# Squares of two of the four outer outputs summed over embeddings by ScalarE, in segments of 64 with its accumulator output, in place of a square on ScalarE and a reduction on VectorE

## The chip, the cores and the metric

The kernel runs on one core of a Trainium2 chip. A core has several engines that work side by side, each with its own in-order queue of instructions: TensorE (PE, matmul), VectorE (DVE), ScalarE (ACT), GpSimd (POOL) and SyncE (SP, which here issues transfers). They share an on-chip memory (SBUF) and an accumulation memory for matmul results (PSUM), and they wait for each other through semaphores. The metric is the device time of one execution in microseconds (us), smaller being better.

## The reference

It is a factorization-machine layer in float32, with 64 embeddings, 512 features, 512 outputs and a batch of 1024:

```python
out_lin = x @ lin_w.T + lin_b
xv = jnp.einsum('bf,efm->bem', x, weight)
zp = jnp.einsum('bf,efm->bem', jnp.square(x), jnp.square(weight))
interaction = 0.5 * jnp.sum(jnp.square(xv) - zp, axis=1)
return out_lin + interaction
```

For each batch row and output column m, the product x times weight is taken for all 64 embeddings e, squared, and summed over e. The sum over e of the squared weights enters through one small product at the end (`zp`).

## The kernel before

**Tiling.** The large product is 1024 x 512 by 512 x (512 outputs x 64 embeddings). The columns are cut into NG = 16 weight groups of 32 outputs x 64 embeddings. In a group the product is done by two levels of a seven-product (Strassen-Winograd) scheme: the outer level makes seven products of blocks, run in the order `ORDER = (1, 6, 2, 7, 4, 5, 3)`, called trees here; inside each tree `tree()` makes seven inner products (`product()`, L433), each as matmuls into a pair of PSUM banks. A tile such as `oa0`, `ob0` or `c_0` is 128 partitions x 2 x 512: G = 2 blocks of batch rows, and in each 512 columns, which are MI = 8 outputs x E = 64 embeddings with the embedding running fastest.

**What a tree does.** Its inner products 5 and 3 go to PSUM tile `b3`, product 1 to `b1`, and ScalarE copies these out: `p5` and `p53` from `b3`, `b2` from `b1` (`copy`, L445, which is L287 in the profile). TensorE then adds products 6, 7 and 4 onto the copied `b2` and product 2 onto `b1`. PLACE sets where each inner product stands on TensorE relative to its tree: product 5 at -6, product 3 at -2, product 1 at 0, up to product 4 at 9, so the trees overlap. Product 3 accumulates onto `b3` only after the copy `p5` has been taken. Then VectorE and GpSimd combine the results into the outer tiles (`outer_psum` and `outer_sbuf`; the two-input adds are L274 in the profile). The inner right-hand sides `t` are made by GpSimd (L426).

**The squares.** When an outer output block is complete, `finish()` (L402) is called for it. This happens in the trees i = 2, 3, 4 and 5, which complete o11, o12, o21 and o22, for each of four positions `pos`. `finish()` squares the tile in place on ScalarE (L289) and then reduces it on VectorE over the 64 embeddings (L296), 128x1024 to 128x16, into the group's accumulator tile `acc`. Tree 4 has its output in a ring of three tiles `c`, tree 3 in `ob0` to `ob3`, trees 2 and 5 in `oa0` to `oa3`. The squares of the weights (`wsq`) take the same two steps in `w_squares()`. At the end of a group `acc` is sent to DRAM; that of the last group is read directly by the additions at L546. After the last group, four banks of closing matmuls (L565) make the `zp` term; VectorE adds it, and the result goes out.

**What sets the order.** Nothing is issued as it is written. Every operation is entered in a `Plan` with a cost for each engine that may run it, its reads and its writes. `Plan.order()` (L62) fixes TensorE's order by key, works latest times back from it, and then simulates all queues: each engine takes the ready operation with the earliest latest time. Some adds may go to VectorE or GpSimd, whichever the planner finds free. The costs are constants in the code: 1.04 for a PSUM copy, 1.07 for a square, 1.14 for a reduction. The resulting sequence is emitted with the engines' in-order queues, so a wrong cost moves no work between engines at run time; it only makes an instruction wait, with all behind it in its queue.

Of the kernel before, what the change touches and what calls it, by code (L numbers as in the profile page):

```python
# [12 lines left out]
AF = mybir.ActivationFunctionType  # L13
# [4 lines left out]
G = 2  # L18
# [5 lines left out]
PE, DVE, ACT, POOL, SP = "PE", "DVE", "ACT", "POOL", "SP"  # L24
# [150 lines left out]
def kernel(  # L175
# [27 lines left out]
    nc = tc.nc  # L203
    NG, NQ, _, NCB, KH, N = weight.shape
# [5 lines left out]
    MI = MG // 4  # L210
    E = N // MI
# [13 lines left out]
    buf = {}  # L225
# [36 lines left out]
    plan = Plan()  # L262
# [3 lines left out]
    def two_input(o, a, b, sub, size=1024, psum=False):  # L266

        costs = {DVE: 0.08 + 1.06 * size / 1024}
        if not psum:
            costs[POOL] = 0.14 + 2.19 * size / 1024  # L270

        def emit(e):
            f = engines[e].tensor_sub if sub else engines[e].tensor_add
            f(o, a, b)  # L274

        return costs, emit
# [7 lines left out]
    def act(o, i, func, reads, writes, cost=1.04):  # L284
        def emit(_):
            if func is None:
                nc.scalar.copy(o, i)  # L287
            else:
                nc.scalar.activation(o, i, func)  # L289

        plan.add({ACT: cost}, emit, reads, writes)

    def reduce(o, i, reads, writes):
        plan.add(
            {DVE: 1.14},
            lambda _: nc.vector.tensor_reduce(  # L296
                o, i.rearrange("p a (m e) -> p a m e", e=E), axis=AX.X, op=ALU.add
            ),
            reads, writes,
        )  # L300
# [17 lines left out]
    for k in range(NK):  # L318
        q, r = divmod(k, KH)
        for g, bank in enumerate(lin_banks):  # L320
            h = g // 2

            def emit(_, k=k, q=q, r=r, g=g, h=h, bank=bank):
                for j in range(G):
                    nc.tensor.matmul(  # L325
                        buf[bank][:, j, :],
                        buf[f"oa{2 * h + q}"][:, r, ts((g * G + j) % (NB // 2), P)],
                        buf[f"ob{q}"][:, r, :],
                        start=(k == 0),
                        stop=(k == NK - 1),  # L330
                    )
# [3 lines left out]
    for g, bank in enumerate(lin_banks):  # L335
        o = ("ob2", "ob3", "c_0", "c_1")[g]
        for j in range(G):
            costs, emit = two_input(buf[o][:, j, :], buf[bank][:, j, :], bias, False, 512, True)
# [3 lines left out]
    def block4(i):  # L342
        return buf[f"X{i}"][:, 0:4, :].rearrange("p (k q) b -> p k (q b)", k=2)
# [8 lines left out]
    def a_ap(n):  # L352
        return buf[a_buf[n]] if n in a_buf else block4(int(n[1]))
# [3 lines left out]
    for i, a, b, sub in ((5, "A21", "A22", 0), (6, "X5", "A11", 1), (7, "A11", "A21", 1), (3, "A12", "X6", 1)):  # L357
        costs, emit = two_input(block4(i), a_ap(a), a_ap(b), sub)
        plan.add(costs, emit, a_parts(a, b), (f"X{i}",), both=True)
    for i in ORDER:  # L360
# [3 lines left out]
        for o, a, b, sub in ((s1, a21, a22, 0), (s2, s1, a11, 1), (s4, a12, s2, 1), (a21, a11, a21, 1)):  # L364
            costs, emit = two_input(o, a, b, sub, 256)
# [36 lines left out]
    def finish(g, i, n, pos):  # L402

        row, col = {2: (0, 0), 3: (0, 1), 4: (1, 0), 5: (1, 1)}[i]
        q, cc = divmod(pos, 2)
        b, m = (row * 2 + q) * G, (col * 2 + cc) * MI
        act(buf[n], buf[n], AF.Square, (n,), (n,), 1.07)
        reduce(buf[acc_name[g]][:, b:b + G, m:m + MI], buf[n], (n,), ((acc_name[g], i, pos),))

# [1 line left out]
    TARGET = {1: "oa", 6: "ob", 2: "oa", 7: "oa", 3: "ob"}  # L411
    RHS = {1: "w11", 2: "w21", 3: "w22", 4: "w21", 5: "T1", 6: "T2", 7: "w12"}
    acc_name = {}
    acc_parts = [(i, pos) for i in (2, 3, 4, 5) for pos in range(4)]

    def tree(s, g, i):
        r = [f"{w(g, RHS[i])}.{c}" for c in range(NCB)]
# [33 lines left out]
        def outer_psum(b, pos):  # L451

            if i == 1:
                copy(f"oa{pos}", b)
            elif i == 5:
                for n in (f"oa{pos}", f"ob{pos}"):
                    whole(n, n, b, psum=True)
                finish(g, i, f"oa{pos}", pos)
            else:
                o = target(pos)  # L460
                whole(o, b, f"{ADDEND[i]}{pos}", psum=True)
                if i in (2, 4, 3):
                    finish(g, i, o, pos)

        def outer_sbuf(b, p, pos):

            if i == 1:
                whole(f"oa{pos}", b, p, psum=True)
            elif i == 5:
                whole(p, b, p, psum=True)  # L470
                for n in (f"oa{pos}", f"ob{pos}"):
                    whole(n, n, p)
                finish(g, i, f"oa{pos}", pos)
            else:
                a, o = f"{ADDEND[i]}{pos}", target(pos)
                z = p if o == a else o
                whole(z, b, p, psum=True)
                whole(o, z, a)
                if i in (2, 4, 3):
                    finish(g, i, o, pos)  # L480
# [41 lines left out]
    last = acc_name[NG - 1]  # L522
# [5 lines left out]
    for g in range(NB // G):  # L528
        n, a = lin_all[g], acc_all[g]
# [12 lines left out]
    def add_acc(g, lo, hi, a, reads):  # L542
        l = buf[lin_all[g]][:, :, lo:hi]
        plan.add(
            {DVE: 0.15 + 1.09 * (hi - lo) / N},
            lambda _: nc.vector.scalar_tensor_tensor(l, a, 0.5, l, ALU.mult, ALU.add),  # L546
            reads + (lin_all[g],), (lin_all[g],),
        )
# [2 lines left out]
        add_acc(g, 0, edge, buf[acc_all[g]][:, :, 0:edge], (acc_all[g],))  # L551
    for g in range(NB // G):
        rows = {0: (2, 3), 1: (4, 5)}[g // 2]
        reads = tuple((last, i, 2 * (g % 2) + c) for i in rows for c in range(2))
        add_acc(g, edge, M, buf[last][:, ts(g, G), :], reads)

    out_dst = out.rearrange("(n p) m -> p n m", p=P)
# [1 line left out]
    for g, bank in enumerate(("b3", "b1", "b2_0", "b2_1")):  # L559
        o = acc_all[g]  # L560
        h = g // 2
        for j in range(G):
            def emit(_, bank=bank, g=g, h=h, j=j):
# [10 lines left out]
            costs, emit = two_input(  # L574
                buf[o][:, j, :], buf[bank][:, j, :], buf[lin_all[g]][:, j, :], False, 512, True
            )
# [37 lines left out]
```

## Time and profile before

| | |
|---|---|
| median of 3 runs | 1438.39 us (1438.19 to 1439.19) |
| profiled execution, its span | 1436.8 us |
| PE busy | 1408.8 us (98%) |
| DVE busy | 1245.7 us (87%) |
| POOL busy | 1149.6 us (80%) |
| ACT busy | 748.8 us (52%) |

The span is the profiled execution's own time from the first to the last instruction. "Busy" is the time in which an engine has an instruction running. In the rows below, a line of the profile names the source line of the kernel, the engine, the operation, the tiles (out<-in, buffer numbers left out), the shapes, how often (x), then busy time and mean duration in ns, and after the second bar the idle time of that engine just before those instructions with what ended it. The chain of waits gives start and duration of each piece of the work that set the end, followed back from the last instruction; "issue" is time in which nothing seen in the profile is waited for.

### The profile page before, as it was taken

The page shows a single profiled execution, that of the slowest core. Times are in us where ns is not written, and L with a number is a line of the kernel's source. Part 1 is how long each engine was busy: PE and PEld are TensorE (multiplying, and loading weights), DVE is VectorE, ACT ScalarE, POOL GpSimd, SP SyncE. Part 2 cuts the span into 40 slices and gives each one's busy share as a digit, 9 for nine tenths or more (in the row PEclk, how much of TensorE's full clock was granted, in tenths as well). Part 3 has the DMA queues.
Part 4 walks back from the last instruction along what each step waited for, and adds up shares of the span by engine and source line. Part 5 has one row for each costly group of instructions (what it writes and reads, how often), then busy time and mean ns, then how long its engine had stood idle before and what let it go on. Part 6 is the DMA issues. An engine that isn't in the chain of part 4 may idle for free.

```text
span 1436.8 us, 10763 instructions
## 1 busy us (share of the span) xinstructions
PE 1408.8 (98%) x3264; PEld 619.3 (43%) x3264; DVE 1245.7 (87%) x1006; ACT 748.8 (52%) x756; POOL 1149.6 (80%) x691
## 2 busy tenths in 40 slices
PE   7999999999999999999999999999999999999998
PEld 3444444444444444444444444444444444444443
DVE  1899898998989899898988989899898888989984
ACT  1465554645545465564556555465554546556441
POOL 6988886878878688896878888687887868889781
PEclk9999999999999999999999999999999999999999
DMA  5311111111111112111111111111111111210221
GB/s 212 117 60 58 48 59 33 59 48 59 59 42 51 33 59 62 46 58 33 59 48 58 59 48 59 33 59 48 58 59 45 53 32 57 60 52 22 88 74 59
DMA packets 40377, 83.54 MB, mean 58 GB/s; under 512 B 18240, under 2 KB 19264, under 8 KB 40320
## 3 DMA queue, kind: packets, MB, share of 16 engines
q1 hardware_dynamic: 39664, 81.54, 18.1%
q10 hardware_dynamic: 576, 1.05, 0.2%
q8 instruction: 27, 0.44, 0.1%
q14 instruction: 30, 0.25, 0.1%
q0 software_dynamic: 80, 0.26, 0.0%
HBM read 76.68 MB, written 6.16 MB: 58 GB/s over the span
## 4 chain that ended last, share of the span: by engine, by line
PE 90%; POOL 4%; DVE 2%; issue 1%; ACT 1%; DMA 1%; DVEq 0%; POOLq 0%; SPq 0%
PE b L438 86%; POOL oa L274 3%; PE b L325 2%; PE b L565 2%; ACT p L287 1%; POOL t L274 1%; DMA ob<-lin_wT 0%; DVE p L274 0%; DMA T1.1_83<-lind 0%; DVE ob L274 0%; DVE w11.1_73 L536 0%; DVE w21.0_76 L274 0%; DVE oa L274 0%; DVE acc L296 0%; DVE w11.0_72 L536 0%
## 5 line engine op out<-in xcount | busy, mean ns | idle before, releaser
L438 PE MATMUL b<-t,X 128*128 128x512 f32 x1792 | 806.2, 592 | 2.0 <-DVE p L274 1.6
L438 PEld LDWEIGHTS b<-t,X 128*128 128x128 f32 x1792 | 340.0, 190 | 431.9 <-issue 415.0
L287 ACT COPY p<-b 128x1024 f32<-128x1024 f32 x224 | 225.6, 1007 | 266.1 <-PE b L438 226.8
L289 ACT ACTIVATE oa<-oa 128x1024 f32<-128x1024 f32 x128 | 131.9, 1054 | 165.3 <-DVE oa L274 90.9
L296 DVE TENSOR_REDUCE w_sum<-wsq 128x16 f32<-128x1024 f32 x128 | 154.8, 1211 | 29.0 <-ACT wsq L289 28.9
L287 ACT COPY b<-b 128x1024 f32<-128x1024 f32 x112 | 111.8, 998 | 91.1 <-PE b L438 85.2
L274 DVE TENSOR_TENSOR p<-b,p 128x1024 f32<-128x1024 f32 x96 | 117.0, 1218 | 43.4 <-PE b L438 43.4
L296 DVE TENSOR_REDUCE acc<-oa 128x16 f32<-128x1024 f32 x128 | 152.0, 1207 | 0.0
L438 PE MATMUL b<-w21.0_76,X 128*128 128x512 f32 x256 | 120.3, 592 | 0.0
L274 POOL TENSOR_TENSOR oa<-oa,p 128x1024 f32<-128x1024 f32 x32 | 102.8, 3212 | 1.8
L289 ACT ACTIVATE c<-c 128x1024 f32<-128x1024 f32 x64 | 67.7, 1058 | 67.8 <-DVE c L274 67.8
L274 POOL TENSOR_TENSOR oa<-p,oa 128x1024 f32<-128x1024 f32 x32 | 75.7, 2365 | 27.2 <-DVE p L274 26.9
L274 DVE TENSOR_TENSOR oa<-b,p 128x1024 f32<-128x1024 f32 x64 | 78.0, 1219 | 11.7 <-PE b L438 10.8
L274 POOL TENSOR_TENSOR c<-c,oa 128x1024 f32<-128x1024 f32 x32 | 75.4, 2357 | 13.8 <-DVE c L274 11.7
L274 POOL TENSOR_TENSOR oa<-oa,ob 128x1024 f32<-128x1024 f32 x32 | 76.4, 2387 | 6.9 <-DVE oa L274 6.9
L274 POOL TENSOR_TENSOR ob<-ob,oa 128x1024 f32<-128x1024 f32 x32 | 76.3, 2384 | 5.5 <-DVE ob L274 5.5
L274 POOL TENSOR_TENSOR t<-w21.0_76,t 128x512 f32<-128x512 f32 x32 | 40.8, 1275 | 48.3 <-PE b L438 48.3
L274 POOL TENSOR_TENSOR ob<-p,ob 128x1024 f32<-128x1024 f32 x32 | 75.7, 2364 | 0.5 <-DVE p L274 0.5
L296 DVE TENSOR_REDUCE acc<-ob 128x16 f32<-128x1024 f32 x64 | 75.9, 1209 | 0.0
L296 DVE TENSOR_REDUCE acc<-c 128x16 f32<-128x1024 f32 x64 | 74.8, 1208 | 1.1 <-ACT c L289 1.1
L438 PEld LDWEIGHTS b<-w21.0_76,X 128*128 128x128 f32 x256 | 48.6, 190 | 61.2 <-issue 61.2
L274 DVE TENSOR_TENSOR ob<-b,oa 128x1024 f32<-128x1024 f32 x32 | 39.1, 1223 | 40.5 <-PE b L438 39.8
(127 smaller groups left out, 2295.9 us busy)
## 6 DMA issues: line engine op xcount, KB each, us to landing
w11.0_72<-weight SPq DMA_DIRECT2D x16, 512.0 KB, 3.7
w11.1_73<-weight SPq DMA_DIRECT2D x16, 512.0 KB, 3.8
w12.0_74<-weight SPq DMA_DIRECT2D x16, 512.0 KB, 3.8
w12.1_75<-weight SPq DMA_DIRECT2D x16, 512.0 KB, 3.8
w21.0_76<-weight SPq DMA_DIRECT2D x16, 512.0 KB, 3.8
w21.1_77<-weight SPq DMA_DIRECT2D x16, 512.0 KB, 4.7
w22a.0_78<-weight SPq DMA_DIRECT2D x8, 512.0 KB, 3.8
w22a.1_79<-weight SPq DMA_DIRECT2D x8, 512.0 KB, 3.8
```

The source lines that it names most:

```text
L274: f(o, a, b)
L287: nc.scalar.copy(o, i)
L289: nc.scalar.activation(o, i, func)
L296: lambda _: nc.vector.tensor_reduce(o, i.rearrange("p a (m e) -> p a m e", e=E), axis=AX.X, op=ALU.add),
L325: nc.tensor.matmul(buf[bank][:, j, :], buf[f"oa{2 * h + q}"][:, r, ts((g * G + j) % (NB // 2), P)], buf[f"ob{q}"][:, r, :], start=(k == 0) ...
L438: nc.tensor.matmul(buf[b][:, j, :], buf[f"X{i}"][:, SLOT[p], ts(j, P)], op, start=first, stop=True, skip_group_check=True,)
L565: nc.tensor.matmul(buf[bank][:, j, :], buf[xe[h, k // KH]][:, k % KH, ts((g * G + j) % (NB // 2), P)], w2_sum[:, k, :], start=(k == 0), st ...
```

## The change

In trees 3 and 4 `finish()` no longer squares the whole tile and reduces it. It cuts the tile into 2 x 8 segments of 64 columns, one for each row block j and output, and squares each with one ScalarE instruction whose accumulator output is written to the output's place in `acc`. Four segments at a time are one entry of the plan, booked at 0.83 us, so a tile makes four entries. Trees 2 and 5, and the squares of the weights, stay as they were. The list of the parts of `acc` that the transfer and the last additions wait for is extended to match.

```diff
@@ finish
         b, m = (row * 2 + q) * G, (col * 2 + cc) * MI
+        if i in (3, 4):
+            for j in range(G):
+                for h in range(2):
+                    def emit(_, j=j, h=h):
+                        for u in range(MI // 2):
+                            v = h * (MI // 2) + u
+                            o = buf[n][:, j, ts(v, E)]
+                            nc.scalar.activation(
+                                o, o, AF.Square,
+                                accum_out=buf[acc_name[g]][:, b + j, m + v:m + v + 1],
+                            )
+
+                    plan.add({ACT: 0.83}, emit, (n,), ((acc_name[g], i, pos, j, h),))
+            return
         act(buf[n], buf[n], AF.Square, (n,), (n,), 1.07)
         reduce(buf[acc_name[g]][:, b:b + G, m:m + MI], buf[n], (n,), ((acc_name[g], i, pos),))
@@
-    acc_parts = [(i, pos) for i in (2, 3, 4, 5) for pos in range(4)]
+    acc_parts = [(i, pos) for i in (2, 5) for pos in range(4)] + [
+        (i, pos, j, h) for i in (3, 4) for pos in range(4) for j in range(G) for h in range(2)
+    ]
@@
-        reads = tuple((last, i, 2 * (g % 2) + c) for i in rows for c in range(2))
+        reads = tuple(
+            (last, *k) for k in acc_parts if k[0] in rows and k[1] // 2 == g % 2
+        )
```

In the changed kernel the segments are line 414. Because the planner makes the order anew from the costs, other instructions on ScalarE, VectorE and GpSimd change places as well; their number and tiles stay the same but for the 128 reductions and 128 whole-tile squares that are gone.

## The prediction

> **What bounds the kernel now.** I read the page first (engines, clock, chain), then the stages, then the chain in order of time.
>
> ```profile
> span 1436.8 us, 10763 instructions
> ...
> PE 1408.8 (98%) x3264; PEld 619.3 (43%) x3264; DVE 1245.7 (87%) x1006; ACT 748.8 (52%) x756; POOL 1149.6 (80%) x691
> ...
> PEclk9999999999999999999999999999999999999999
> ```
>
> TensorE is busy for 98% of the span at a granted clock in the top tenth throughout. ScalarE (ACT), the engine that gets the new work, has the most room on average: 52%. An average hides where work is bunched, so I cut out one of the 16 weight groups:
>
> ```profile
> core 0: us, PE busy (x) PEld busy (x) DVE busy (x) ACT busy (x) POOL busy (x), PEclk, DMA share, GB/s
> ...
> 207.13:292.32 85.19, 84.37 (x197) 37.15 (x196) 76.25 (x62) 46.51 (x48) 69.91 (x42) 1.00 0.17 52
> ```
>
> A group lasts 85.19 us, 84.37 of it matmul. With seven trees in a group that is 84.37 / 7 = 12.05 us of PE per tree. The other 0.8 us is one stop, which the chain shows:
>
> ```profile
> 207.13 1.00 ACT p L287
> 208.13 0.04 issue
> 208.17 79.25 PE b L438 x184
> 287.42 0.03 POOLq L274
> 287.45 0.59 POOL t L274
> 288.04 3.30 POOL oa L274
> 291.34 0.02 issue
> 291.36 0.02 ACT oa L289
> 291.38 0.94 issue
> 292.32 1.00 ACT p L287
> 293.33 0.04 issue
> ...
> 1404.63 27.48 PE b L565 x64
> ```
>
> At the end of each group POOL's last `oa` add ends at 291.34. Only then can ACT square that `oa`, and the copy of `b3` into `p5` at 292.32 stands behind this square in ACT's queue. PE waits for the copy. The wait seen from PE, summed over 16 groups:
>
> ```profile
> L438 PE MATMUL b<-w11.1_73,X 128*128 128x512 f32 x64 | 31.7, 618 | 13.4 <-ACT p L287 13.4
> ```
>
> So what can be gained in the groups is at most 13.4 us; what can be lost has no such bound, since the copies that PE waits for and the squares share one in-order queue.
>
> **The change, part by part.** Removed: per group, the four `c` squares of tree 4 and the four `ob` squares of tree 3, with a reduction each.
>
> ```profile
> L289 ACT ACTIVATE c<-c 128x1024 f32<-128x1024 f32 x64 | 67.7, 1058 | 67.8 <-DVE c L274 67.8
> L289 ACT ACTIVATE ob<-ob 128x1024 f32<-128x1024 f32 x64 | 67.6, 1059 | 4.8 <-POOL ob L274 1.6 <-DVE ob L274 0.5
> ...
> L296 DVE TENSOR_REDUCE acc<-ob 128x16 f32<-128x1024 f32 x64 | 75.9, 1209 | 0.0
> L296 DVE TENSOR_REDUCE acc<-c 128x16 f32<-128x1024 f32 x64 | 74.8, 1208 | 1.1 <-ACT c L289 1.1
> ```
>
> DVE loses 75.9 + 74.8 = 150.7 us, 9.4 of its 76.25 per group. I credit nothing for it beyond the 13.4 us bound: in the chain above, DVE isn't what PE waits for, and a group can't be shorter than its 84.37 us of matmul. What hides DVE's work now is that matmul stream; it has 8.9 us of DVE idle per group before, more after.
>
> Added on ACT: 128 sets, each cut into G x MI = 16 squares of 128x64, so 2048 squares. In the built program each is followed by an instruction of its own that reads the accumulator out, so 4096 new instructions stand where 128 stood. The planner books 0.83 us for four squares, 0.2075 each. No DMA is issued or moved past anything else's data: SP's transfers keep their buffers, and POOL and PE keep the same instructions.
>
> *Steps of the large ones.* ACT overlaps neighbours a little, so I take start to start:
>
> ```profile
> 246.75 0.99 ACT L287 COPY p<-b 128x1024 f32<-128x1024 f32 x1
> 247.64 1.06 ACT L289 ACTIVATE oa<-oa 128x1024 f32<-128x1024 f32 x1
> ...
> 265.36 1.06 ACT L289 ACTIVATE wsq<-w11.0_72 128x1024 f32<-128x1024 f32 x1
> 266.31 1.04 ACT L289 ACTIVATE wsq<-w22b.1_81 128x1024 f32<-128x1024 f32 x1
> ```
>
> A copy takes 0.89 us of the queue (I use 0.90), a square 0.95 of its 1.06: some 0.10 us of a record lies under the next.
>
> *One segment, c us: a square of 64 and its read.* The trace has no ACT instruction this short and no accumulator read, so I bound both. Low: 0.95 x 64/1024 = 0.06 for the square with no fixed part, and 0.10 for the read, the piece of a record that the square alone would have hidden; c = 0.16. High: the nearest short rows are DVE's.
>
> ```profile
> L546 DVE SCALAR_TENSOR_TENSOR T1.1_83<-w22a.1_79,T1.1_83 128x960 f32<-128x960 f32 x1 | 1.1, 1145 | 0.0
> L546 DVE SCALAR_TENSOR_TENSOR w21.1_77<-acc,w21.1_77 128x64 f32<-128x64 f32 x1 | 0.2, 216 | 0.0
> ```
>
> From 960 to 64 elements the record falls by 929 ns over 896 elements, 1.04 ns each, so 216 - 66 = 150 ns is fixed. Two such records end to end, 0.216 + 0.216, with 0.02 for the hand-over (the "issue" pieces of the chain), give c = 0.45. I take one short record plus one fixed part, c = 0.216 + 0.150, less a little for overlap: **c = 0.36**. I lean to the high end because the read needs the finished sum of the square just ahead, and the next square can't add into the accumulator before it is read: the overlap that the 1024-wide rows show should be mostly lost.
>
> The Trainium skill ("ScalarE: Activation LUTs", section What ACT_TABLE_LOAD costs) gives an ACTIVATE with immediate operands 186 ns + 0.833 ns per element, neighbours overlapping by 93 ns. For 1024 elements that is 1039 ns and a step of 946, and the trace agrees (1058 and 950). It has no price for the read; taken as one more instruction of one element, an estimate from that page is 146 + 94 = 240 ns for c, and the sum below would come to about 1459. "Perfetto Trace Analysis" of the Trainium skill, section Optimizing Scalar/DVE Operations, puts about 93 ns of fixed busy time on a ScalarE operation on SBUF: 3968 more instructions would be an estimated 369 us more on ACT, 748.8 + 369 = 1118 of 1437, so read on the average that rule sees no loss; no row here has a short ACT instruction to test it.
>
> *Where it stands in ACT's queue.* I counted the changed program's ACT queue from one `p5` copy to the next, that is, per tree of 12.05 us of PE. From group 1 on, in order of (PSUM copies, whole squares, segments): trees 1 to 3 of the order have (4,1,20), (4,1,12), (3,3,0); then (3,5,0), (3,2,16), (3,3,48), and across the group's boundary (3,1,32). The segments of trees 4 and 3 are bunched: 100 of a group's 128 lie in three neighbouring stretches, (3,3,48), (3,1,32), (4,1,20). In these ACT has 10 copies x 0.90 + 5 squares x 0.95 + 100 c = 13.75 + 100 c, while PE has 3 x 12.05 = 36.15 us. They are level at **c = 0.224**. Above that each further 0.01 us costs 1 us per boundary, since the copies of `b3` and `b1` stand behind the segments and PE soon has nowhere to write. (Over a whole group ACT has 23 x 0.90 + 16 x 0.95 + 128 c = 35.9 + 128 c, level with 84.37 only at 0.38: the average says there is room, the stretch says there isn't.)
>
> *Sum.* At c = 0.36: 13.75 + 36.0 - 36.15 = 13.6 us late per boundary. Each stop also costs part of the 1.00 us copy that PE then waits for in full; I add 0.6, so 14.2. There are 15 boundaries between groups: 213. The present stop of 13.4 / 16 = 0.84 lies at the same boundary and is swallowed: 15 x 0.84 = 12.6 off. After the last boundary 108 segments remain with 3 copies and 4 squares, 108 x 0.36 + 2.7 + 3.8 = 45.4 us. Beside them PE has what follows product 5 of the last tree: its six other products and the four of the tree before that `PLACE` sets behind it, 10 x 12.05 / 7 = 17.2 us, and the closing 27.48 us of L565, together 44.7: 0.7 us remain. 1436.8 - 12.6 + 213 + 0.7 = 1638; the median of the runs is 1438.39, 1.6 over the profiled span: **1639.5; I say 1640**.
>
> At the high end, c = 0.45, the boundary costs 22.6 + 0.6 = 23.2, x 15 = 348, and the tail 108 x 0.45 + 6.5 - 44.7 = 10.4: 1436.8 - 12.6 + 348 + 10.4 + 1.6 = 1784. At the low end the stretch fits and the result is the first rival.
>
> **Rivals.**
> *The segments fit (c up to 0.22).* Mechanism: ACT keeps ahead in the bunched stretches, the squares at the group boundary are cut into pieces of four between which the `p5` copy can stand, and the 0.84 us stop shrinks. At most 13.4 us go; I take 10: 1428. For: the planner's own 0.2075, and 52% ACT. Against: it needs two instructions for less than one short DVE record (216 ns). It decides at c = 0.224; below it the change is faster.
> *Cheap read (c from 0.23 to 0.30).* The square and the read pipeline like the 1024-wide rows, only with a fixed part each. At 0.24: 1.6 + 0.6 = 2.2 per boundary, 33 in all, less the 12.6: 1459. At 0.30: 7.6 + 0.6, 123 in all: 1549. For: the large squares do hide 0.10 us of each other. Against: nothing shows that a read hides under the square whose sum it takes.
> *Dearer than two short records (c over 0.45).* A read that waits for the square's write to be acknowledged and blocks the next, so that each segment costs more than 0.45 of queue. Over 1784; for it speaks only that no row excludes it.
>
> **How the numbers follow.** Fits 0.15; cheap read 0.22; forecast (c 0.30 to 0.45, 1549 to 1784) 0.56; dearer 0.07. A measurement of this kernel tells 0.2%, about 2.9 us, from no change. That is met only close to c = 0.22, so same is 0.03; faster 0.14, slower 0.83. The range leaves out the first rival, the lowest edge of the second and the last: 1450 to 1785. It is wide because a hundred segments stand in each stretch: each 10 ns of the unknown c is 15 us of the time.
>
> **What would show it.** Right: line 414's segments with a read each, 0.30 to 0.45 us start to start; ACT busy without gaps from the tree 5/3 stretch to tree 6 of the next group; PE's idle time, ended by ACT's copies of `b3` and `b1`, 10 to 20 us per group around the boundary and little in trees 7 and 4; DVE's busy time down by about 150 us and its idle time up. Wrong: a start to start under 0.22 with PE at 84.4 us per group; PE waiting for DVE or POOL rather than for ACT; stops that lie in trees without segments.

## The result, and the profile after

The changed kernel takes 1445.86 us (median of 4 runs, 1445.6 to 1446.25), the kernel before, on the same chip, 1438.54. The ratio is 1.005, with a 95% interval of 1.0037 to 1.0064 (later intervals are of the same kind): slower by half a per cent. That is the forecast direction, but 194 us short of the forecast size and 4 us below the lower edge of the range.

The page of the changed kernel, its head and the rows that answer to those shown before:

```profile
span 1443.8 us, 14564 instructions
...
PE 1410.8 (98%) x3264; PEld 619.8 (43%) x3264; DVE 1141.2 (79%) x878; ACT 1091.8 (76%) x4724; POOL 1161.9 (80%) x691
...
L414 ACT ACTIVATE c<-c 128x64 f32<-128x64 f32 x1024 | 245.7, 247 | 51.6 <-DVE c L274 51.6
L414 ACT ACTIVATE ob<-ob 128x64 f32<-128x64 f32 x1024 | 248.0, 260 | 1.9 <-DVE ob L274 1.9
L414 ACT ACTIVATION_READ_ACCUMULATOR ob<-ob 128x1 f32 x1024 | 210.7, 206 | 0.0
...
L414 ACT ACTIVATION_READ_ACCUMULATOR c<-c 128x1 f32 x1024 | 197.7, 193 | 0.0
```

The read after each segment is there, 2048 of them. ACT rises from 748.8 to 1091.8 us, DVE falls by 104.5 us, not by the 150.7 of the removed reductions. The other 46 us are a balance in the group view: some of VectorE's adds take longer in the new order, others less. `w12.1_75<-w22b.1_81,w12.1_75` takes 3368 ns in the mean (before 1213) and `T1.0_82<-w12.0_74,w11.0_72` 2849 (before 1763), but `T2.0_84<-w22b.0_80,T1.0_82` 1337 (before 3364). What differs is which engine starts first. In the kernel before, a `w12.1` add began at 280.07 us, just ahead of a GpSimd add, and took 1.21 us; in the changed kernel it began at 275.44 under a GpSimd add that had begun at 274.53, and took 3.37, to 1.08 us after the end of GpSimd's.

The records of a square and its read (247 to 260 and 193 to 206 ns) don't add up to what a segment costs. That is read from starts, in ACT's timeline:

```profile
640.49 0.25 ACT L414 ACTIVATE ob<-ob 128x64 f32<-128x64 f32 x1
640.64 0.20 ACT L414 ACTIVATION_READ_ACCUMULATOR ob<-ob 128x1 f32 x1
640.73 0.25 ACT L414 ACTIVATE ob<-ob 128x64 f32<-128x64 f32 x1
```

Square to read 0.15 us, read to next square 0.09: a segment takes **0.24 us** of the queue. (The median over all is 0.239.) That is above the 0.2075 booked and the 0.224 at which the prediction set the turn, and far below its 0.36.

The chain of waits, one group:

```profile
682.82 15.52 PE b L454 x37
698.34 0.02 issue
698.36 1.06 ACT c L414 x8
699.43 0.89 ACT p L287
700.32 1.87 ACT c L414 x16
702.20 0.10 issue
702.30 0.91 ACT c L414 x7
703.21 0.73 ACT b L287
703.94 0.11 issue
704.05 1.00 ACT p L287
705.06 0.96 ACT c L414 x8
706.02 0.95 ACT wsq L289
706.97 4.47 ACT c L414 x38
...
711.74 0.89 ACT p L287
712.63 1.91 ACT oa L289 x2
714.54 0.91 ACT b L287
715.45 4.70 ACT c L414 x39
...
720.16 1.06 ACT c L414 x8
721.22 0.90 ACT p L287
722.12 0.04 issue
722.17 1.98 PE b L454 x4
```

Before, POOL's `oa` add and one square stood ahead of the `p5` copy. Now it is ACT itself: from the moment tree 4's first `c` tile is ready (698.36) it works with hardly a pause through all 64 `c` segments, five copies and three whole squares, 22.9 us, and only then reaches the copy at 721.22. 64 segments at the booked 0.2075 would have ended 64 x 0.032 = 2.1 us sooner, ahead of PE's need. The stop, by PE's row:

```profile
L454 PE MATMUL b<-w11.1_73,X 128*128 128x512 f32 x64 | 31.7, 619 | 16.6 <-ACT p L287 16.6
```

16.6 us instead of 13.4. The 7.1 us of span are made up so: the boundaries of the chain stand at 123.36 and, seven groups on, at 722.17, 85.54 us a group (before 122.97 and 719.39, 85.20); by the last boundary this makes 1320.94 against 1315.79, **5.15 us**. From there to the end it is 122.9 us against 121.0, the other **1.9**, in the last tree. PE's row above has 3.2 of the 5.15 us; most of the rest are smaller waits some 80 us into a group.

### The profile page after: what moved, and what is told of

Same layout as the page of the kernel before. It is cut to its first block, busy times and chain, and to the rows that moved or that the text cites. A ratio compares the mean times of both kernels' runs of the same rounds, so it can differ in the third digit from the quotient of the medians.

```text
span 1443.8 us, 14564 instructions
## 1 busy us (share of the span) xinstructions
PE 1410.8 (98%) x3264; PEld 619.8 (43%) x3264; DVE 1141.2 (79%) x878; ACT 1091.8 (76%) x4724; POOL 1161.9 (80%) x691
## 3 DMA queue, kind: packets, MB, share of 16 engines
q10 hardware_dynamic: 576, 1.05, 0.2%
## 4 chain that ended last, share of the span: by engine, by line
PE 69%; ACT 26%; DVE 3%; DMA 1%; issue 1%; POOL 0%; DVEq 0%; SPq 0%; ACTq 0%; POOLq 0%
PE b L454 65%; ACT c L414 16%; ACT p L287 4%; ACT oa L289 2%; PE b L325 2%; PE b L583 2%; ACT b L287 2%; DVE c L274 1%; ACT wsq L289 1%; DMA w21.1_77<-weight 1%; DVE oa L274 1%; DVE w_sum L296 1%; DMA ob<-lin_wT 0%; DVE p L274 0%; POOL oa L274 0%
## 5 line engine op out<-in xcount | busy, mean ns | idle before, releaser
L287 ACT COPY p<-b 128x1024 f32<-128x1024 f32 x224 | 225.1, 1005 | 88.3 <-PE b L454 70.3
L414 ACT ACTIVATE c<-c 128x64 f32<-128x64 f32 x1024 | 245.7, 247 | 51.6 <-DVE c L274 51.6
L414 ACT ACTIVATE ob<-ob 128x64 f32<-128x64 f32 x1024 | 248.0, 260 | 1.9 <-DVE ob L274 1.9
L414 ACT ACTIVATION_READ_ACCUMULATOR ob<-ob 128x1 f32 x1024 | 210.7, 206 | 0.0
L414 ACT ACTIVATION_READ_ACCUMULATOR c<-c 128x1 f32 x1024 | 197.7, 193 | 0.0
L274 DVE TENSOR_TENSOR ob<-b,p 128x1024 f32<-128x1024 f32 x32 | 39.2, 1224 | 86.9 <-PE b L454 86.9
L274 POOL TENSOR_TENSOR c<-c,oa 128x1024 f32<-128x1024 f32 x32 | 88.6, 2770 | 13.4 <-DVE c L274 11.3
L274 POOL TENSOR_TENSOR oa<-oa,p 128x1024 f32<-128x1024 f32 x32 | 89.2, 2788 | 5.9 <-DVE p L274 3.5
```

The lines of the kernel that those rows point to most:

```text
L414: nc.scalar.activation(o, o, AF.Square, accum_out=buf[acc_name[g]][:, b + j, m + v:m + v + 1],)
```

## The experiments

Two readings had to be told apart. *A*: a segment costs ACT more than the plan booked, and the order made from the wrong price puts the boundary's copy too late. *Rivals*: VectorE's and GpSimd's new order is to blame; or ACT's work is too much whatever the order; or the stop is a matter of order alone, and VectorE's relief buys nothing.

**Without the reads.** The segments stay; without their sums, `acc` is set to zero at the start (not shown in the cut). In the trace every engine has the instructions of the changed kernel in the same order, but for the reads and the zeros.

```diff
-                            nc.scalar.activation(
-                                o, o, AF.Square,
-                                accum_out=buf[acc_name[g]][:, b + j, m + v:m + v + 1],
-                            )
+                            nc.scalar.activation(o, o, AF.Square)
```

> The changed kernel's order, but the segments of 64 give no accumulator output, so no reads; the sums of trees 3 and 4 are left out (zeros instead). Theory A (a segment with its read takes 0.24 us of ScalarE where the plan booked 0.2075, and the stretch before the group's boundary comes late): a segment takes 0.15 us, ScalarE reaches the p5 copy in time, the stop at each boundary falls from 1.13 us to under 0.3, and the time is about 1425. Rival B (VectorE's new order runs into GpSimd's adds, c<-c,oa 2357 -> 2770 ns, and makes the c tiles late): the stops stay, about 1444.

1431.01 us, ratio 0.9947 (0.9932 to 0.9963). A segment takes 0.146 us start to start, a group 84.64 (mean of 14, between the first `w11.1` matmuls). With nothing changed but ACT's load, the change turns from slower to faster: A holds and the rival of VectorE's order can't be the cause of the loss. But 1425 was expected and 6 us are left; the next run shows a part of them.

**The right price.**

```diff
-                    plan.add({ACT: 0.83}, emit, (n,), ((acc_name[g], i, pos, j, h),))
+                    plan.add({ACT: 1.0}, emit, (n,), ((acc_name[g], i, pos, j, h),))
```

> The changed kernel with the plan's price for four segments raised from 0.83 to 1.0 (0.25 each, measured 0.24). Theory A: the planner no longer puts so many segments ahead of the copies, the boundary stop goes below 0.3 us, about 1425 to 1428, faster than the kernel before. Rival C (ScalarE has too much work in trees 4, 3 and 1 whatever the order, 13.75 + 24 us against 36.15): still slower than before, 1440 to 1450.

1435.02 us, ratio 0.9977 (0.9967 to 0.9986). The same work as in the changed kernel, at 0.24 us a segment, is 0.2% *faster* than before once the planner knows what it costs. ACT's work isn't too much. It fell short of 1425 to 1428, and the chain of this kernel at a boundary shows a part of the reason:

```profile
285.84 1.21 DVE p L274
287.05 1.13 DVE T2.0_84 L274
288.18 3.31 DVE ob L274
291.49 0.02 issue
291.51 0.04 ACTq L287
291.55 0.04 issue
291.59 1.02 ACT p L287
292.61 0.04 issue
292.66 2.41 PE b L454 x5
```

Another wait took the place of the old. VectorE's add `ob<-ob,p` reads the `p` tile that ACT's copy is to overwrite, so the copy, and PE, wait for it. VectorE has this add 15 times in the kernel before too; there it began at 286.84, ahead of the add `T2.0`, took 2.28 us and ended 3.2 us before the boundary's copy began. Here it stands behind `T2.0`, starts under a running GpSimd add and lasts until 291.49. So this wait, too, is a matter of order. It costs PE 0.24 us at this boundary: the last four matmuls ahead of it begin at 290.70 and take 0.43 us each, the next begins at 292.66. A group takes 84.92 us here, 0.55 over the 84.37 of matmul in a group; the rest are smaller waits inside the group. The kernel without reads has the same chain (`ob` 3.31 us, then the copy at 290.99).

**Twice the segments.** Each as two squares of 32, both read into the same element (the call itself, cut here, only moves in by one level).

```diff
-                            o = buf[n][:, j, ts(v, E)]
+                            for half_seg in range(2):
+                                o = buf[n][:, j, ts(2 * v + half_seg, E // 2)]
```

> The changed kernel with each segment as two squares of 32 columns, each with a read (the first half's sum is overwritten and so left out). Theory A: 2 x (0.15 - 0.027 + 0.09) = 0.43 us a segment; ScalarE is then late by some 20 us at each boundary, 1745 by the prediction's sum (13.75 + 42.6 - 36.15 + 0.6 = 20.8 per boundary) and up to 1790 if stops elsewhere in the group add. Rival D (stops do not scale with ScalarE's work, because the squares move to where there is room): under 1500.

2074.18 us, in one run. Both numbers under A were too low, since the price was: 0.567 us a segment, not 0.43. The timeline has the extra:

```profile
639.85 0.23 ACT L415 ACTIVATE c<-c 128x32 f32<-128x32 f32 x1
639.99 0.19 ACT L415 ACTIVATION_READ_ACCUMULATOR c<-c 128x1 f32 x1
640.08 0.21 ACT L415 ACTIVATE c<-c 128x32 f32<-128x32 f32 x1
640.20 0.19 ACT L415 ACTIVATION_READ_ACCUMULATOR c<-c 128x1 f32 x1
640.42 0.23 ACT L415 ACTIVATE c<-c 128x32 f32<-128x32 f32 x1
```

After a read that goes to a new element the next square follows in 0.09 us; after one that goes to the same element as the read before, in 0.22. What makes the additional 0.13 us was not isolated. At 0.567 the prediction's sum gives 13.75 + 56.7 - 36.15 + 0.6 = 34.9 per boundary, 15 x 34.9 = 524, with a tail of 108 x 0.567 + 6.5 - 44.7 = 23: 1436.8 - 12.6 + 524 + 23 + 1.6 = 1973. It is still 101 short. The granted clock in this run was 0.879 of full, which no term has. Stops do scale with ACT's work (rival D falls); how much of the 101 us is clock and how much stops elsewhere in the group stays open.

**The price that was predicted.** A further square of 24 columns behind each segment, into a scratch tile `pad` that is made beforehand.

```diff
+                            nc.scalar.activation(pad[:, 0:24], bias[:, 0:24], AF.Square)
```

> The changed kernel with a further small square (24 columns of a constant tile into a scratch tile, no accumulator) behind each segment, which makes a segment cost ScalarE about 0.24 + 0.10 + 0.02 = 0.36 us, the price that the prediction took; order and results as in the changed kernel. By the prediction's sum 1640; by the sum with stops elsewhere in the group up to 1655; more than that where the granted clock falls as it did with the doubled segments (0.879 there). If the sum overcounted at every price as it did at 0.24 (1459 against 1445.9), some 13 less.

1653.58 us, ratio 1.1496 (1.1473 to 1.1519); the segment with its additional square takes 0.352 us. At that price the prediction's sum gives 1627, so it is 27 us too low. Its groups are 99.04 us apart, 13.8 more than before, where the sum had 13.4 - 0.84 = 12.6; and the end lies 13.2 us farther from the last boundary than before, where the sum had nothing. PE stands still for 9.0 us a group, not for 13.4; another 5.7 us a group go into matmuls that run slower. The granted clock was 0.957 of full in this run, and PE is busy for 1495.8 us with the same 3264 matmuls (before 1408.8). The prediction has no term for that, and how much of the 27 us it makes stays open. But ACT has next to no idle time from 28 us ahead of a boundary to 28 us behind it, PE waits there mostly for ACT's copies, and the time comes out within 27 of 215 us. So the prediction missed mainly by its price, not by its mechanism.

**One tree at a time.** `if i in (4,):` and `if i in (3,):` for `if i in (3, 4):`, the other tree as before.

> Segments in tree 4 alone (the c tiles, 64 segments a group); tree 3 squares and reduces as before. Theory A: the stretch that comes late runs from the first c square to the p5 copy of the next group and holds only c segments, so the whole loss at the boundaries is here: stops of 1.1 us, about 1444 to 1446.

> Segments in tree 3 alone (the ob tiles); tree 4 squares and reduces as before. Theory A: the ob segments come after the late copy and find room in trees 1, 6 and 2, so the boundary keeps the old stop of 0.98 us; the last tree still has them at its end, up to 2 us: 1438 to 1441.

Tree 4 alone: 1445.85 us, ratio 1.0052 (1.0037 to 1.0067), all that the change loses. As the chain suggests, its 64 `c` segments suffice. Tree 3 alone: 1443.30, ratio 1.0034 (1.0021 to 1.0047), where 1438 to 1441 was expected. The boundary keeps its old stop, and a second one comes up, which I hadn't foreseen, at the copy of `b1`:

```profile
210.71 2.33 POOL ob L274
213.04 0.02 issue
213.06 1.58 ACT ob L414 x13
...
216.04 0.92 ACT b L287
216.95 0.04 issue
217.00 15.29 PE b L454 x35
```

The mispriced `ob` segments are put ahead of another copy. The two losses don't add; the planner makes a different order in each case.

**The last group as before.** `if i in (3, 4) and g < NG - 1:`, with the old reduction in the last group.

> The changed kernel, but in the last group trees 3 and 4 square and reduce as before. Of the 7.1 us by which the changed span is longer, 2.0 lie behind the last boundary (1315.8 to the end 120.97 before, 122.90 after). If they come from the segments in the last tree, with nothing of PE behind to hide them but the closing products, they go: about 1444, and the boundaries stay at 85.54 a group. If the last 2 us come from the order of the adds, the time stays at 1446.

1442.79 us, ratio 1.0028 (1.0017 to 1.0038). Boundaries 85.55 apart, the last at 1321.03, and the closing matmuls begin 88.3 us behind it, against 90.8 in the changed kernel. The tail is the last tree's segments.

**The order alone.** No segments at all; the plan's price of a whole square in the kernel before.

```diff
-        act(buf[n], buf[n], AF.Square, (n,), (n,), 1.07)
+        act(buf[n], buf[n], AF.Square, (n,), (n,), 1.5)
```

> The kernel before, no segments, with only the plan's price of a square in the outer outputs raised from 1.07 to 1.5, so that the order changes and no work does. Theory A says nothing of it. If the stop of 0.98 us at the boundary is a matter of order alone, it goes here too and the time is about 1426 without any work moved from VectorE; if it takes VectorE's relief to remove it, the time stays at 1438.

> The kernel before with squares priced at 1.5, beside the other two on one chip: 1426, ratio 0.991.

1426.03 and 1425.55 us, ratios 0.9913 (0.9899 to 0.9926) and 0.9907 (0.9894 to 0.9921): the fastest kernel of this study, and VectorE has slightly *more* to do in it: under the new price the planner also gave it 17 adds that GpSimd had before (1006 and 1023 instructions, GpSimd's 691 and 674). So it isn't order alone that changed, though no work left VectorE. The rows:

```profile
PE 1408.5 (99%) x3264; PEld 619.5 (43%) x3264; DVE 1262.4 (89%) x1023; ACT 744.2 (52%) x756; POOL 1139.6 (80%) x674
...
L438 PE MATMUL b<-w11.1_73,X 128*128 128x512 f32 x64 | 30.2, 594 | 1.1 <-ACT p L287 1.1
```

The stop of 13.4 us is 1.1, the one at the start. The last `oa` square still stands ahead of the boundary's copy in ACT's queue, but POOL's add releases it sooner: it begins at 202.86 for a boundary at 206.64, 3.8 us ahead, where it was 2.0 before (206.16 and 208.17).

**VectorE's relief alone**, with the old order's price and with the better one: the 128 reductions and their sums left out, the squares whole.

```diff
-        reduce(buf[acc_name[g]][:, b:b + G, m:m + MI], buf[n], (n,), ((acc_name[g], i, pos),))
+        if i in (2, 5):
+            reduce(buf[acc_name[g]][:, b:b + G, m:m + MI], buf[n], (n,), ((acc_name[g], i, pos),))
```

> The kernel before, squares of trees 3 and 4 whole on ScalarE as they were, but their 128 reductions on VectorE and so their sums left out (zeros instead); the planner orders anew. It has all the relief of VectorE that the change gives and none of ScalarE's price. If VectorE's relief (150.7 us of work) is worth something by itself, the boundary stop goes and the time is about 1425; if only the order counts, it is no better than the kernel before with squares priced at 1.5, which took 1426.0. Over 1436: the relief is worth nothing.

> The kernel before without the 128 reductions of trees 3 and 4 (their sums left out) and with squares priced at 1.5: the relief of VectorE and the better order together, with no price on ScalarE. If VectorE's relief has a worth beyond order: under 1425. If not: 1426 or more, and the whole aim of the change is worth nothing in this kernel.

1434.92 us, ratio 0.9964 (0.9950 to 0.9978), and 1431.29, ratio 0.9951 (0.9938 to 0.9965). Even without the segments' price, the relief brings less than the other price of a square does: leaving the reductions out of the reordered kernel makes it slower, 1431 against 1426. The second kernel's chain has the same `ob` add behind `T2.0` on VectorE, 3.30 us, ahead of the copy at 290.44. The planner made a new order for each of the two, so what the relief is worth in a fixed order was not measured.

**Both prices.** Segments at 1.05 and whole squares at 1.5.

> The changed kernel with four segments priced at 1.05 and the remaining whole squares of outer outputs at 1.5 in the plan. If segments cost nothing once the order knows their price, it equals the kernel before with squares at 1.5: 1426, a ratio of 0.991. If the segments keep a price of their own (stops of PE behind POOL's t tiles, as with price 1.0), 1430 to 1436, slower than that kernel.

1429.48 us, ratio 0.9935 (0.9923 to 0.9948): the best that segments with their sums reached here, and 4 us behind the reordered kernel without them. It lies just under 1430 to 1436. Its groups are 84.66 us apart, against 84.37 in the reordered kernel, and its boundary's copy, at 290.32, waits for the same `ob` add behind `T2.0`. So most of the 4 us go with the order again; whether the segments have a price of their own stays open.

## Why the prediction was wrong, point by point

- **The bound** (PE, one stop per group from a copy queued on ACT): right, and the reordered kernel shows the gain's limit to have been real: 1.1 of the 13.4 us are left, and 12.4 us of time went.
- **The price of a segment**: this step failed. "The overlap that the 1024-wide rows show should be mostly lost" is what the timeline refutes: the read starts 0.15 us after its square, whose record is 0.25, and the next square 0.09 after the read, whose record is 0.19 to 0.21. Two records that add up to 0.44 or more take 0.24. The low end, 0.16, and the high, 0.45, did hold it; the choice between them went by a row of another engine. The Trainium skill ("ScalarE: Activation LUTs", section What ACT_TABLE_LOAD costs) has 186 ns + 0.833 ns per element for an ACTIVATE, with 93 ns of overlap, and no price for the read. The prediction's estimate from it, 146 + 94 ns, agrees with the trace part by part: 0.146 and 0.093 us.
- **Which case**: the second rival, the cheap read, is what came, with a chance of 0.22. Its time at 0.24 was 1459.
- **The sum at the right price** is 13 us too high. It had 2.2 - 0.84 = 1.36 us more per boundary; 0.34 were measured. It summed three stretches with 100 segments, of which only the 48 of the first stand ahead of the copy that comes late; the stretch that counts begins when the first `c` is ready and holds the 64 `c` segments alone. It also had nothing for the tail, where 1.9 us were found. At higher prices the error turns: the sum rises by 15 us for each 10 ns of a segment, the runs by some 18.5 between 0.24 and 0.352, in part with a lower clock.
- **The sign "ACT busy without gaps"** was seen: from 698.4 to 745.0, around a boundary, ACT is busy for 46.60 of 46.60 us. Yet PE stood for only about 1 us. A full ACT doesn't stop PE; what stops it is work ahead of a copy that PE needs next.
- **The threshold**: a segment costs 0.24, the turn was put at 0.224, and the direction came out right, by 0.016 us and so in part by luck, since 0.36 was expected. But the right price in the plan turns the same work into a gain. So the turn belongs to one order, not to ACT's work. The prediction treated the order as fixed by the work and didn't ask what the planner would do with the true price.
- **Order as rival**: the prediction had the planner's 0.2075 as a price that could be true, not as the cause of the order. That was the gap: of the time lost and won in these runs, the larger part hangs on two constants, 0.83 and 1.07.
- **VectorE's relief** was credited with nothing beyond the bound. The runs agree as far as they go: no kernel with the relief beats the reordered one without it. About a third of the relief went, on balance, into slower adds (104.5 us instead of 150.7), and in the orders that come with it an add that holds the `p` tile stands late. The relief in a fixed order was not measured.

## What to carry to other kernels

Where a planner orders in-order queues ahead of time, a moved operation changes two things: the engine's load and the order of everything. Price the new operation from a trace before judging the move, and compare with the old kernel under other prices, since a gain or loss of a per cent may be the order alone. Measure a short instruction's price from start to start; neither its record nor a row of another engine gives it. A stretch to be summed begins where its first operand becomes ready and ends at the instruction that someone waits for; check it again at every price, since it can grow.

## What the runs showed of the hardware

**After a stop TensorE's matmuls can run at half speed.** In the kernel at 0.352 us a segment, this came after a stop of 3.30 us:

```profile
225.18 1.88 PE L456 MATMUL b<-w22b.0_80,X 128*128 128x512 f32 x4
230.36 3.78 PE L456 MATMUL b<-w11.1_73,X 128*128 128x512 f32 x4 [3.30 <-ACT p L288]
233.93 2.91 PE L456 MATMUL b<-t,X 128*128 128x512 f32 x4
236.68 1.88 PE L456 MATMUL b<-w11.0_72,X 128*128 128x512 f32 x4
```

Four take 3.78 us instead of 1.88, the next four 2.91, then all is as before. The mean granted clock between 229 and 238 us was 0.62, and 1.00 between 240 and 260. Stops of about 1 us, as in the changed kernel, left the clock at 1.00. The length of the stop alone doesn't decide it. In the run at 0.352, all 20 stops of 2.39 to 2.68 us were followed by matmuls at half speed for some 3.4 us; of the 15 stops of 3.3 us only 10 were, and of the 25 between 0.5 and 1.5 us none. "TensorE: Matmul & The Clock Gate" of the Trainium skill, section Part 1, has the clock halved after an idle window of some 3.4 us and restored after about as long a busy one. Here stops of 2.4 us already did it, and stops of 3.3 us did not always.

**VectorE waits for a GpSimd add that started first.** In the kernel before, 15 of VectorE's two-input adds of 128x1024 from SBUF start while no GpSimd add runs, and each takes 1.21 or 1.22 us. The 128 that start under one end 1.08 to 1.16 us after the end of GpSimd's, and take up to 3.37.
